# Layer 2's cross attention: outputs by token from centred folded values, six heads' maxima as the bias of the exponential, steps in a written order

## The chip, the core and the metric

The kernel runs on one core of a Trainium2 chip. The core's engines work from queues of their own: TensorE (PE in the profile; PEld are its weight loads) for matrix products, VectorE (DVE), ScalarE (ACT) and GpSimd (POOL) for the rest, and SyncE (SP), which issues most DMAs. Products land in PSUM, which has eight banks of 512 float32 per partition; all else lies in SBUF.

The metric is the device time of one execution in microseconds, as the median over runs. Everything is float32.

## The reference

A small decoder of four layers; every layer is a cross attention to a context, then a mixture of experts. The change concerns the attention of layer 2. Cut to what matters, with 8 sequences of 256 tokens of width 128 (2048 tokens, 16 tiles of 128), 64 context rows per sequence, 16 heads of width 64:

```python
q = split_heads(einsum('bnd,df->bnf', norm(x), Wq)) * 64 ** -0.5
k, v = split(einsum('bmc,cf->bmf', context, Wkv), 2)
k = concatenate((null_k, k)); v = concatenate((null_v, v))     # one null key and value per head
attn = softmax(einsum('bhid,bhjd->bhij', q, k))                # 65 numbers per head
out = einsum('bnf,fd->bnd', merge_heads(attn @ v), Wout)
mu, var = mean(out), variance(out)
out = (out - mu) * rsqrt(var + 1e-6) * ln_scale + ln_bias
x = x + tanh(gate) * out
```

`norm` is a layer norm over the 128 numbers of a token. What follows is layer 2's feed-forward part: two routings to 8 experts (cosine logits, a mask, a softmax over the chosen), an attention whose projections are mixed by the first routing's gates, and experts weighted by the second's.

## The kernel before

x stays in SBUF as 16 tiles of 128 tokens by 128, in four chunks of four tiles (`TPC`). Layer 2's keys and values are *folded*: with `Wq` and the keys multiplied beforehand (`G`, per sequence 128 x 16 heads x 64) the scores of a tile are one product of its normed, turned x with `G`; with the values and `Wout` multiplied beforehand (`U`) the output of a tile is one product of its weights with `U`. `folds` makes G and U in eight pieces (k = 0 to 7, two heads each): `keys_values(k)`, then `fold`. Five calls of it are spread over layer 1's experts (`l1_ffn`), the others run before `l2_xattn`. `constants2` does the same with the null key and value (`gn`, `nvu`).

`l2_xattn` then goes through the tiles:

- `normed(c)` norms a chunk and turns it (`xTs`).
- `weights(t)`, two tiles ahead: scores of 16 heads x 64 in two PSUM banks (`sc2`) and the null scores (`sn`) on PE; the maximum per head, the subtraction from all 1024 scores and from the null scores, on DVE; two exponentials on ACT; sums and reciprocal on DVE; the division (a multiplication by `rs`) on POOL.
- `turned(t)`: eight turns on PE, copied by ACT to `pTs` (two banks of kind `l2m` are shared by all such uses), and one turn of the null weights.
- `summed(b)`, for two tiles of one sequence: the output as 128 features x 256 tokens (`py2`), copied (`yT2`), turned back to tokens (`yt2`), statistics with `bn_stats` and `bn_aggr`, copied (`yr2`), `rstd` by a power on POOL, the norm on DVE, scale and bias on POOL, the addition to x on DVE.

Within the loop, at tiles 8 to 14, stands part of the next layer's work for chunks 0 and 1: `normed2` and `logits2` (norm, turn, cosine logits), `routed2` (mask and gates), `spread2` and `loaded2` (the gates go to HBM and come back spread over 128 partitions into the place of `G`). `l2_ffn` begins with `queries(0)`, which multiplies x's normed chunk by these gates.

The order on each engine: where the code says nothing, a scheduler of the framework orders the instructions of a stage when the program is built, by its own estimates. In a block with `tc.manual_schedule` every engine takes its instructions in the order of the code; layers 1 and 3 have such blocks, layer 2's attention has none. Waits between engines are semaphores that the framework sets from what each instruction reads and writes. `power` is the POOL instruction at line 219. `evac` copies PSUM to SBUF by ACT and DVE in turns. `over(a, n)` repeats a number along the last axis.

Of the kernel before, what the change touches and what calls it, by code (L numbers as in the profile page):

```python
# [20 lines left out]
AF = mybir.ActivationFunctionType  # L21
# [3 lines left out]
P = 128  # L25
# [3 lines left out]
NCH = 4  # L29
# [8 lines left out]
def tile_flamingo(ctx: ExitStack, tc: tile.TileContext, a: dict, out: bass.AP):  # L38
# [1365 lines left out]
    def normed2(c):  # L1404


        st = mk(small, [P, TPC, 6], "st")
        t = slice(c * TPC, (c + 1) * TPC)
        for k in range(TPC):
            v.bn_stats(st[:, k, :], xs(c)[:, k, :])  # L1410
            v.bn_aggr(r2["mv"][:, c * TPC + k, :], st[:, k, :])
        pw = mk(small, [P, 2, TPC], "pw")
        v.tensor_scalar(pw[:, 0], r2["mv"][:, t, 1], 1e-5, None, ALU.add)
        v.tensor_scalar(pw[:, 1], r2["mv"][:, t, 1], 1.0 + 1e-5, 1e-10, ALU.mult, ALU.add)
        power(r2["pw"][:, :, t], pw, 2 * TPC)
        xn = mk(act, [P, TPC, D], "xn")
        ln_apply(xn, xs(c), r2["mv"][:, t], r2["pw"][:, 1, t])
        return xn
# [26 lines left out]
    def routed2(half, i):  # L1445
# [7 lines left out]
        v.tensor_tensor(lo, lo, under(sgt[:, i, :], HT), ALU.subtract)  # L1453

# [5 lines left out]
        top = top_mask(lo, 2)  # L1460
        v.tensor_tensor(top, top, over(m, E), ALU.mult)
# [30 lines left out]
    def l1_l2():  # L1492

# [11 lines left out]
        with psum(4, 2), tc.tile_pool(name="l2w", bufs=1) as wp:  # L1505
# [35 lines left out]
            def constants2():  # L1541
# [14 lines left out]
                s.activation(gn, pn2, AF.Copy, scale=0.125)  # L1556
# [23 lines left out]
            def fold(k, kT, vd):  # L1580
                G, U = Gs[k // 4], Us[k // 4]
# [10 lines left out]
                for h in range(2):  # L1592
                    evac(G[:, :, 2 * (k % 4) + h, :], pg[:, h])
                for b4 in range(2):
# [11 lines left out]
            def folds():  # L1606


                with behind(l1["ph"]):
                    kv = keys_values(0)  # L1610
                yield
                for k in range(8):
                    nxt = keys_values(k + 1) if k < 7 else None
                    fold(k, *kv)
# [3 lines left out]
            def l2_xattn(lp):  # L1618

                p2s = [t.rearrange("p (h m) -> p h m", h=16) for t in (wa2[:, 0:1024], wa2[:, 1024:2048])]  # L1620
                p2s.append(vds[0].rearrange("p b t m -> p (b t m)").rearrange("p (h m) -> p h m", h=16))
                p2Ts = [wa2[:, 2048 * i : 2048 * (i + 1)].rearrange("p (k q) -> p k q", k=8) for i in (1, 2)]
                xTs, pTs, pnTs = {}, {}, {}

                def normed(c):
                    xTs[c] = mk(wp, [P, CW], "t2k", bufs=2)
                    pt = misc([P, CW], "pt")
                    xn = layernorm(c)
# [895 lines left out]
```

## Time and profile before

| what | value |
|---|---|
| median of six runs | 1112.53 us (1109.11 to 1125.4) |
| the profiled execution, its own time | 1101.95 us |
| its span, first to last instruction | 1100.2 us |
| mean granted TensorE clock | 0.93 |
| PE busy | 973.2 us (88%) |
| PEld busy | 550.4 us (50%) |
| DVE busy | 629.8 us (57%) |
| ACT busy | 451.2 us (41%) |
| POOL busy | 312.8 us (28%) |
| HBM traffic | 50.50 MB read, 8.26 MB written |

The span begins with the first instruction and ends with the last. Busy time is that in which an engine had an instruction running; PE's is drawn a little long, since products overlap and their ends are modelled. The profile has a view by windows of time, a view of groups of instructions (by line, engine, operation and tiles, with what ended the idle time ahead of them), a timeline, and a chain of waits: from the last instruction back, at each step to whatever released it. In these views the names of tiles that share an arena are those of the arena: `arena_a` stands for the weights `pa`, the turned weights and the folding's inputs; `t2k` for the turned x. A float32 product of 512 columns shows as two instructions.

Layer 2's attention proper lies between about 576 and 694 us of the span, the folding of pieces 4 to 7 directly ahead of it, layer 2's experts behind it.

### The profile page before, as it was taken

To read this page: it belongs to the slowest core of one execution; us is meant where nothing else is said; L and a number is where in the kernel's file an instruction comes from. 1 tells how busy PE (TensorE), PEld (TensorE's weight loads), DVE (VectorE), ACT (ScalarE), POOL (GpSimd) and SP (SyncE) were. 2 spreads that over 40 slices of the span, in tenths; PEclk is the share of its full clock that TensorE was granted. 3 is DMA by queue.
4 is the path that set the end of the run, shared out by engine and by line. 5 is a ranking of instruction groups with operands and counts; after the bars stand their busy time and mean duration, and the time that the engine had idled before them with its cause. 6 is when DMAs were issued, how large, how long until landed. Compare 5 with 4: busy or idle time off the path is not lost.

```text
span 1100.2 us, 14774 instructions
## 1 busy us (share of the span) xinstructions
PE 973.2 (88%) x5090; PEld 550.4 (50%) x5090; DVE 629.8 (57%) x1690; ACT 451.2 (41%) x875; POOL 312.8 (28%) x348
## 2 busy tenths in 40 slices
PE   5898989889999999899998988979998699887896
PEld 3557756644444344334454646434444244555684
DVE  4475435565746563343428997844757755555454
ACT  3633533354444455632234434322203444452353
POOL 2128761141100001000003555230541610322554
PEclk9889999999999998898999998989999899985698
DMA  9403321031010100300210000714431203000243
GB/s 252 89 13 52 75 57 32 25 96 38 3 39 4 41 2 2 115 0 1 77 39 1 1 0 7 244 38 154 154 114 54 101 22 133 1 20 11 45 85 101
DMA packets 59337, 64.31 MB, mean 58 GB/s; under 512 B 11096, under 2 KB 48512, under 8 KB 59008
## 3 DMA queue, kind: packets, MB, share of 16 engines
q1 hardware_dynamic: 54016, 54.14, 16.0%
q0 software_dynamic: 3968, 8.13, 3.7%
q10 hardware_dynamic: 1280, 1.09, 0.5%
q8 instruction: 42, 0.69, 0.3%
q14 instruction: 31, 0.25, 0.1%
HBM read 50.50 MB, written 8.26 MB: 53 GB/s over the span
## 4 chain that ended last, share of the span: by engine, by line
PE 65%; DVE 17%; POOL 6%; ACT 5%; issue 4%; DMA 2%; SPq 1%; ACTq 0%; POOLq 0%; DVEq 0%
PE gur L770 4%; PE st L1126 4%; PE pymT L1814 4%; PE yr L795 3%; PE sc L1032 2%; PE phm L1905 2%; DVE nmx L1039 2%; PE o L1145 2%; PE pqmT L1814 2%; PE yt L1349 2%; PE gu L746 2%; PE pvmT L1814 2%; PE sc L1640 2%; PE ph L1301 1%; PE pu L1597 1%
## 5 line engine op out<-in xcount | busy, mean ns | idle before, releaser
L219 POOL TENSOR_TENSOR rstd<-rstd,mhalf 128x4 f32<-128x4 f32 (+1 forms) x37 | 35.2, 950 | 377.6 <-DVE rstd L234 335.6
L1039 DVE TENSOR_REDUCE nmx<-sc 128x4 f32<-128x1024 f32 x64 | 76.5, 1220 | 56.5 <-PE sc L1032 56.4
L1130 ACT ACTIVATE pT<-st 128x1024 f32<-128x1024 f32 x64 | 64.5, 1023 | 63.7 <-PE st L1126 48.3
L770 PE MATMUL gur<-arena_a,xrT 128*128 x184 | 62.2, 462 | 0.9 <-ACT xrT L764 0.7
L612 POOL DMA_INDIRECT xr<-xk,dp_src x46 | 46.8, 1017 | 42.0 <-DVE lg_m L287 28.3
L1814 PE MATMUL pymT<-G,arena_b 128*128 128x512 f32 x104 | 47.2, 598 | 1.5 <-DVE G L1806 1.3
L1661 POOL TENSOR_TENSOR arena_a<-arena_a,rs 128x1024 f32<-128x1024 f32 x16 | 30.5, 1904 | 58.7 <-DVE rs L1660 42.3
L787 DVE COPY aTr<-pta 128x256 f32<-128x256 f32 x46 | 19.5, 424 | 47.6 <-PE pta L785 47.6
L795 PE MATMUL yr<-arena_a,aTr 128*128 (+1 forms) x276 | 38.4, 275 | 0.1
L770 PEld LDWEIGHTS gur<-arena_a,xrT 128*128 128x128 f32 x184 | 31.7, 190 | 13.3 <-ACT xrT L764 1.6
L1640 PE MATMUL sc<-G,t2k 128*128 128x512 f32 x64 | 34.2, 626 | 4.6 <-DVE rs L1659 3.7
L778 ACT ACTIVATE sgr<-gur 128x352 f32<-128x352 f32 x46 | 21.3, 463 | 37.1 <-PE gur L770 37.1
L612 POOL DMA_INDIRECT xn<-yg,dp_rows x32 | 30.3, 947 | 21.5 <-issue 7.9
L795 PEld LDWEIGHTS yr<-arena_a,aTr 128*128 128x128 f32 (+1 forms) x276 | 34.4, 191 | 0.3 <-DVE aTr L787 0.3
L1126 PE MATMUL st<-arena_a 32*128 32x512 f32 x128 | 34.2, 672 | 0.0
L275 DVE SCALAR_TENSOR_TENSOR x<-yt,tg,x 128x512 f32<-128x512 f32 x16 | 12.0, 748 | 37.6 <-PE yt L1354 21.6
L612 POOL DMA_INDIRECT xr<-z,dp_src x30 | 28.5, 950 | 15.4 <-issue 8.1
L1814 PEld LDWEIGHTS pymT<-G,arena_b 128*128 128x128 f32 x104 | 19.1, 190 | 26.1 <-issue 14.3
L2226 POOL TENSOR_TENSOR arena_a<-arena_a 128x256 f32<-128x256 f32 x18 | 14.0, 775 | 60.4 <-DVE arena_a L2225 60.4
L1032 PE MATMUL sc<-arena_b 32*128 32x512 f32 x128 | 30.2, 666 | 0.8 <-DVE yr L804 0.4
L1126 PE MATMUL st<-arena_b,l1k 32*128 32x512 f32 x128 | 30.9, 631 | 0.0
L1905 PE MATMUL phm<-nT,arena_b 128*128 128x512 f32 x64 | 29.9, 622 | 0.0
(544 smaller groups left out, 2395.8 us busy)
## 6 DMA issues: line engine op xcount, KB each, us to landing
G<-gd SPq DMA_DIRECT2D x40, 512.0 KB
xe<-gd SPq DMA_DIRECT2D x8, 512.0 KB
arena_a<-in_L_ffn_exp_wgu_dram SPq DMA_DIRECT2D x2, 1408.0 KB
yg<-yr SPq DMA_DIRECT2D x10, 256.0 KB
arena_a<-qkT SPq DMA_DIRECT2D x32, 64.0 KB
arena_a<-in_L_xattn_Wkv_dram SPq DMA_DIRECT2D x1, 2048.0 KB
y<-yr SPq DMA_DIRECT2D x6, 256.0 KB
x<-in_x_dram SPq DMA_DIRECT2D x4, 256.0 KB
```

Of the source, the lines that this page charges most:

```text
L219: g.tensor_tensor(dst, src, mhalf[:, 0:n], ALU.pow)
L612: return g.indirect_dma_start(out=dst, out_offset=None, in_=src, in_offset=bass.IndirectOffsetOnAxis(ap=idx, axis=0))
L770: pe.matmul(gu[:, h, 0:352], xrT[t], wgu[:, bass.ds(e + 1, 1), h * 352 : h * 352 + 352].rearrange("p e f -> p (e f)"), start=True, stop=True,)
L795: pe.matmul(y, aT[0:n, i, :], wd[0:n, bass.ds(e + 1, 1), i, :].rearrange("p e d -> p (e d)"), start=(i == 0), stop=(i == 2),)
L1032: pe.matmul(sc[:, i].rearrange("p h t -> p (h t)"), qd[r, k, tokens(qt)], kb[r, k, b].rearrange("p h t -> p (h t)"), start=True, stop=True,)
L1039: v.tensor_reduce(nmx[:, qt, 2 * u : 2 * u + 2, 2 * k : 2 * k + 2], sc, AX.X, ALU.max, negate=True)
L1126: pe.matmul(st[:, i], kd[r, k, b, kt * P : (kt + 1) * P], qb[r, k, :, tb], start=True, stop=True)
L1130: s.activation(pT[n, u], st, AF.Exp)
L1640: pe.matmul(sc[:, 8 * k : 8 * k + 8, :].rearrange("p h m -> p (h m)"), xT[:, q], Gs[k][:, b].rearrange("p h m -> p (h m)"), start=True, st ...
L1661: g.tensor_tensor(pa, pa, over(rs, S2), ALU.mult)
L1814: last_pe[0] = pe.matmul(pq, w[:, e, :], xe[e // 4][:, e % 4, :], start=(e == 0), stop=(e == E - 1))
L1905: pe.matmul(ph, w1p[:, e, :], nTc(c), start=True, stop=True)
```

## The change

It does five things.

1. **Folded values less their means.** The mean over the 128 output columns is taken off `wo` (and so off `U` and `nvu`), in `folds`. The output then has mean zero, and its variance is the mean of its squares: `bn_stats` and `bn_aggr` go.
2. **Outputs by token.** `summed(t)` takes the turned weights as the stationary side and U as the moving one, for one tile at a time: the output is tokens x 128, four tiles in one bank `y`. The copies and turns behind it go. ACT's `squared` sums the squares, `rstd` takes the power per pair, `back` scales from PSUM on DVE and adds to x on POOL. The bias is added to x in `normed`.
3. **Six heads' maxima as the bias.** For heads 0 to 5 ACT takes the exponential from PSUM with the negated maximum as its bias and sums it as it goes (`accum_out`); for heads 6 to 15 and the null weights, which now lie behind them in one stretch of `pa`, DVE subtracts as before and ACT takes one exponential.
4. **Steps of fixed order.** `l2_xattn` stands in a `manual_schedule` block. Step t holds the pieces of tiles t+2, t+1, t, t-1 and a finished pair, in one written order; norms, logits, routing and the spread of gates are cut into pieces (`routed2` becomes a generator, `normed2` two functions) and appended to the end of chosen steps (`plan`). The norms of chunks 0 and 1 stand ahead of the block.
5. **Last folding within.** `fold` is cut in two; the values of k = 6 and 7 are folded in steps -2 and -1.

The null scores and the turned null weights share one bank (`null`). `gn` changes sign, so that `min` with the negated maxima serves. The diff, cut to its core:

```diff
             def folds():
                 with behind(l1["ph"]):
                     kv = keys_values(0)
+                wm = mk(small, [P, 8], "wm", bufs=1)
+                row_sum(wm, wo)
+                v.tensor_scalar(wm, wm, 1.0 / D, None, ALU.mult)
+                g.tensor_tensor(wo, wo, over(wm, D), ALU.subtract)
                 yield
...
+                    fold_scores(k, kT)
+                    if k < 6:
+                        fold_values(k, vd)
...
+                def scores(t):
...
+                    pe.matmul(sn(t), xT[:, q], gn, start=True, stop=True)
...
+                def maxima(t):
...
+                    v.tensor_reduce(nm, sc, AX.X, ALU.max, negate=True)
+                    v.tensor_tensor(nm, nm, sn(t), ALU.min)
+                    v.tensor_tensor(pa[:, HB:16, :], sc[:, HB:16, :], over(nm[:, HB:16], S2), ALU.add)
+                    v.tensor_tensor(pn, nm, sn(t), ALU.subtract)
+
+                def exps(t):
...
+                    for h in range(HB):
+                        s.activation(
+                            pa[:, h, :], sc[:, h, :], AF.Exp, bias=nm[:, h : h + 1], accum_out=rs[:, h : h + 1]
+                        )
+                    pl = pas[t % 3][:, HB * S2 : 1040]
+                    s.activation(pl, pl, AF.Exp)
+
+                def divided(t):
...
+                    row_sum(rs[:, HB:16], pa[:, HB:16, :])
                     v.tensor_tensor(rs, rs, pn, ALU.add)
                     v.reciprocal(rs, rs)
+                    g.tensor_tensor(pn, pn, rs, ALU.mult)
                     g.tensor_tensor(pa, pa, over(rs, S2), ALU.mult)
...
+                def summed(t):
+
+                    yt = y[:, t % TPC, :]
                     for k in range(8):
+                        pe.matmul(yt, pTs[t % 2][:, k, :], Us[k // 4][:, t // 2, k % 4, :], start=(k == 0), stop=False)
+                    pe.matmul(yt, pnTs.pop(t), nvu, start=False, stop=True)
+
+                def squared(t):
+                    junk = mk(lp, [P, D], "junk2")
+                    s.activation(junk, y[:, t % TPC, :], AF.Square, scale=D**-0.5, accum_out=vs[:, t : t + 1])
...
+                def back(b):
                     yn = mk(lp, [P, 2, D], "yn")
+                    for t in (2 * b, 2 * b + 1):
+                        v.scalar_tensor_tensor(
+                            yn[:, t % 2, :], y[:, t % TPC, :], vs[:, t : t + 1], lns, ALU.mult, ALU.mult
                         )
                     xb = x[:, 2 * b : 2 * b + 2, :]
+                    g.tensor_tensor(xb, xb, yn, ALU.add)
...
+                for k in (6, 7):
+                    plan[k - 8].append(lambda k=k: fold_values(k, vds[k % 2]))
+                for c, t in ((2, 1), (3, 4)):
+                    stats, apply, turn = normed(c)
...
+                def late(c):
+                    stats, apply = normed2(c)
...
+                    def turn_in():
+                        got.extend(logits2(c, apply(), 0, misc, nsq))
+                        got[0]()
+
+                    return stats, turn_in, lambda: got[1]()
+
+                for c, t in ((0, 6), (1, 10)):
+                    for k, f in enumerate(late(c)):
+                        plan[t + k].append(f)
+                routing = routed2(0, 0)
+                for t in (12, 13, 14):
+                    plan[t].append(lambda: next(routing, None))
...
+                plan[15].append(first_half)
+                for t in range(-2, NT + 2):
                     if t + 2 < NT:
+                        scores(t + 2)
+                    done = t - 2 if t >= 3 and t % 2 else None
+                    if 0 <= t + 1 < NT:
+                        divided(t + 1)
+                    if done:
+                        rstd(done // 2)
+                    if 0 <= t < NT:
+                        turned(t)
+                    if t + 2 < NT:
+                        maxima(t + 2)
+                        exps(t + 2)
+                    if 0 <= t - 1 < NT:
+                        summed(t - 1)
+                        squared(t - 1)
+                    if done:
+                        back(done // 2)
+                    for f in plan[t]:
+                        f()
...
+                with tc.manual_schedule(engines=all_four):
+                    l2_xattn(xp)
```

`first_half` is the old `t == 14` branch: `spread2` for chunks 0 and 1, then `loaded2` for both. `turned(t)` turns the null weights first, then the eight blocks, and copies all three results on ACT.

## The prediction

> **What bounds it now.** I read the page's 40 slices first: PE is nine tenths busy nearly everywhere, and DVE reaches nine tenths only in the stretch from 576 to 690 us, the attention of layer 2, which the change rewrites. So I cut that stretch and the start of the next layer into windows (columns: length, then busy time and instructions of PE, PEld, DVE, ACT, POOL, then granted clock, DMA share, GB/s):
>
> ```profile
> 576.00:590.00 14.00, 9.21 (x27) 4.52 (x28) 10.18 (x18) 3.81 (x6) 2.18 (x3) 0.90 0.00 0
> 590.00:635.00 45.00, 43.95 (x209) 29.10 (x207) 40.03 (x90) 22.66 (x49) 24.65 (x26) 0.99 0.00 1
> 635.00:684.00 49.00, 41.03 (x179) 24.78 (x180) 41.87 (x128) 21.15 (x47) 26.32 (x27) 0.92 0.00 1
> ...
> 716.00:733.00 17.00, 10.07 (x33) 3.83 (x32) 4.61 (x8) 3.73 (x7) 7.52 (x9) 0.70 0.15 51
> ```
>
> The filling (576 to 590) leaves PE 5 us idle; then PE is full, and DVE nearly; after 635 neither is full. The chain of waits, cut to 590 to 625 us, says which of the two paces the full part (start, length, what):
>
> ```profile
> by line: PE sc L1640 33.3%; PE py L1685 29.6%; PE tp L1675 18.7%; PE py L1686 5.4%; PE sn L1647 3.8%; PE tn L1678 2.3%; PE yt L1691 1.9%; ACT arena_a L1676 1.7%; PE pt L1630 1.2%; ACT yr L1698 1.0%; issue 0.5%; DVE rstd L1700 0.5%; ACT pn L
> ...
> 605.32 3.46 PE py L1685 x16
> 608.77 0.62 PE py L1686 x2
> ```
>
> It is PE. One pair of tiles costs it 2 x (1.72 scores + 0.13 null scores + 0.95 turns + 0.11) + 4.08 outputs + 0.22 = 10.1 us, 5.06 a tile. The exponentials of tiles 0 to 10 (L1655) start at 581.07 and 634.48: 5.34 a tile. The last five tiles take 43.9 us, to 678.34: routing falls there. Then the groups of 574 to 700 us (count, busy us, mean ns, idle before and releaser):
>
> ```profile
> L287 DVE TENSOR_REDUCE m<-sc 128x16 f32<-128x1024 f32 x16 | 19.4, 1214 | 4.7 <-PE sc L1640 4.7
> L316 DVE TENSOR_REDUCE rs<-arena_a 128x16 f32<-128x1024 f32 x16 | 19.4, 1210 | 2.0 <-ACT arena_a L1655 2.0
> L1653 DVE TENSOR_TENSOR arena_a<-sc,m 128x1024 f32<-128x1024 f32 x16 | 19.2, 1199 | 0.1
> L1661 POOL TENSOR_TENSOR arena_a<-arena_a,rs 128x1024 f32<-128x1024 f32 x16 | 30.5, 1904 | 58.7 <-DVE rs L1660 42.3 <-DVE pn L1654 4.0 <-DVE tk_m L305 3.4
> L1698 ACT COPY yr<-yt 128x256 f32<-128x256 f32 x8 | 2.9, 367 | 1.2 <-DVE st L1695 1.2
> ```
>
> Three passes over 1024 numbers fill DVE. The last line matters later: ACT's copy of `yt` waits for DVE's statistics of the same `yt`, though neither writes what the other reads. Two readers of one PSUM bank go one after the other here.
>
> **The change, part by part.** PE: the sixteen `py` products of 256 columns and the two turns become per tile 18 instructions on 128 columns. `pu` (L1597) has that form: 16 in 1.98 us, 0.124 each. So 2.23 a tile against (4.08 + 0.22) / 2 = 2.15: PE stays at 1.85 + 1.06 + 2.23 = 5.14 a tile. PE gains nothing, so what can be won is idle time only: the 5 us of filling and about 17 us of the last tiles (43.9 - 5 x 5.34).
>
> DVE: heads 6 to 15 alone are shifted and summed, 640 of 1024 numbers. A 1024-wide pass is 1.13 us from start to start (619.19 to 620.33), about 0.07 of it fixed, so 640 take 0.74 (0.80 to its end). Statistics leave (`bn_stats`, `bn_aggr`), `yn` takes one pass per tile from PSUM, and the addition to x goes to POOL. That removes this collision, POOL and DVE in one stretch of the timeline (the usual addition takes 0.43):
>
> ```profile
> 628.21 1.90 POOL L1661 TENSOR_TENSOR arena_a<-arena_a,rs 128x1024 f32<-128x1024 f32 x1
> 628.29 2.10 DVE L1710 TENSOR_TENSOR x<-x,yn 128x256 f32<-128x256 f32 x1 [0.20 <-POOL yn L1708]
> ```
>
> ACT: the copies `yT` and `yr` leave (0.37 each, per pair). Six exponentials of 64 columns with a bias and a sum come in, then one of 656 (0.73, by 1.058 for 1024), and a square with its sum (0.42). What one small exponential costs is not in the trace; the nearest rows are these:
>
> ```profile
> 14.16 0.41 ACT L413 ACTIVATE sg<-arena_b 64x256 f32<-64x256 f32 x1 [2.77 <-DMA arena_b<-in_ctx_dram]
> 14.48 0.18 ACT L413 ACTIVATION_READ_ACCUMULATOR sg<-arena_b 64x1 f32 x1
> 14.69 0.42 ACT L413 ACTIVATE sg<-arena_b 64x256 f32<-64x256 f32 x1
> ...
> 761.30 0.40 ACT L1869 ACTIVATE pam<-pam,mm 128x128 f32<-128x128 f32 x1 [3.30 <-DVE mm L1868]
> 761.60 0.19 ACT L1869 ACTIVATION_READ_ACCUMULATOR pam<-pam,mm 128x1 f32 x1
> 761.70 0.49 ACT L1869 ACTIVATE pam<-pam,mm 128x256 f32<-128x256 f32 x1
> ```
>
> Each sum is a second instruction. The lower pair is the same exponential with bias, 0.40 apart at 128 columns, 0.34 at 64; the upper is 0.53 apart at 256 columns, 0.37 at 64 and about 0.45 with a bias. I take 0.39, six in 2.34.
>
> [...]
>
> **The fixed order makes a loop.** In every step each engine takes: DVE `divided(t+1)`, then `maxima(t+2)`; ACT the copies, `exps(t+2)`, `squared(t-1)`. DVE can't sum tile t+1 before ACT ends `exps(t+1)`, can't start the maxima of t+2 before that sum, and ACT can't start `exps(t+2)` before the shifted heads are written, since both read the first bank of `sc`. Once round: sum 0.74, add 0.09, reciprocal 0.16, maximum 1.13, minimum 0.09, shift 0.80 = 3.01 on DVE, 2.34 + 0.73 = 3.07 on ACT, two waits of 0.04: 6.15 us, above PE's 5.14 and the old 5.34. (Between 5.8 and 6.5 by the price of the small exponentials.) Fifteen rounds lead from the end of the first tile's exponentials to the last's: 92.2.
>
> Added to single rounds: in odd steps `back` reads bank `y` on DVE behind ACT's `squared` in the same bank (0.45 after the exponentials) and takes 0.6 for two tiles (L642, 0.346 for 128 columns); the next sum is queued behind it: 1.1 in five rounds, 5.5. The planned pieces stand last in a step, so what they wait for holds the next step's work. Applying the norm in step 5: four passes behind `back`, partly against POOL's addition, 1.5. `turn_in` in steps 7 and 11: PE's turns wait for that pass, and the next scores (1.85) queue behind them on PE: 3.1 each. `logits` in step 8: PE's second turn waits for an ACT copy behind `exps(10)`, so scores 11 come 2.8 late. Step 12: the first piece of routing waits on DVE for those logits and POOL's power (1.65), with the sum of tile 14 behind it: 4.4. Together 14.9. Sum 92.2 + 5.5 + 14.9 = 112.6, against 97.3 now (exponentials end at 582.13 and 679.40): **+15.3**. Bounds: 87 with stalls covered by idle DVE, to 118.
>
> Start: the four `pu` groups of k = 6, 7 (4 us on PE) go into the filling. The last `pg` ends at 573.1 less 2.0, G is copied by 572.5, scores, maximum and shift (2.0 + 2.1) and exponentials (3.0) end near 579.6: **-2.5**.
>
> Tail (same view; the spread of the gates, their loads, the first gated product):
>
> ```profile
> 684.63 1.08 SPq L1478 DMA_DIRECT2D gd<-arena_a  x2
> ...
> 686.17 4.14 SPq L1487 DMA_DIRECT2D G<-gd  x8
> ...
> 690.17 0.69 DVE L1806 TENSOR_TENSOR G<-G,nT 128x512 f32<-128x512 f32 x1 [0.58 <-DMA G<-gd]
> ```
>
> Now 10.8 us pass from the last exponentials to the first gated product; PE works on outputs under the loads. After, the spread stands at the end of step 15: `back` 1.05, routing 2.0, sum 1.0, POOL 2.2, turns 1.1, outputs of tile 14 2.3, spread 0.9, copies 0.9 = 11.4, and 4.8 from the last copy to the product as now (685.41 to 690.17): 16.2, **+5.4**; 0 if the pieces overlap. Only tile 15's outputs lie under these loads, so SP's queue starts them later against the end.
>
> Layer 2's experts: PE idles 7 of 17 us at 716 to 733, because x's last tiles are ready at 698.8, 8.6 after the first gated product, and their norm, routing and squares (POOL, 721) come late. After, x is ready before that product: 0 to 7 won, I take **-4**, the middle, since the program's own order there decides. Taken at nothing: the means of `wo` (1.21 on DVE, 1.90 on POOL, the L316 and L1661 forms) run under the matmuls of layer 1's experts, where POOL is idle; without that cover 3.1, and the first `pu` would be late.
>
> Sum: +15.3 - 2.5 + 5.4 - 4 = +14.2. The profiled execution took 1101.95 (span 1100.2), 1% under the median 1112.53; on its own time 1116, on the median **1126 us**.
>
> **Rivals.** *PE paces.* If the small exponentials cost near 0.22, or started at the minimum, the loop would fall below 5.14 and PE would set 15 x 5.14 = 77 plus 8 of planned matmuls: 85 against 97.3, -12.3; with -2.5 + 5.4 - 4 it is -13, **1099**. For it: DVE does 3.5 a step instead of 5.3, and loses no time to POOL. Against: the 0.40 row, and `yr` waiting for `st`. *Stalls covered.* The loop holds, but DVE's 3 us of idle time in every round take in the planned pieces: 92.2 + 5.5 - 97.3 = 0.4; with the other three terms -0.7, **1112**. *Table loads.* If the square needs another table than the exponential, two loads of 1.28 a tile stand in the loop: 16 x 2.57 = 41 more, **1167**. Against it: the squares at 10.89 follow a tanh at 10.78 with no load between. This is slower still than my forecast. The changed steps plainly do what they say; no rival is needed for that.
>
> **Chances.** Loop with stalls 0.49, covered 0.28, PE paces 0.20, table loads 0.03. About 1% (11 us) is what a measurement here can tell from no change. The first case lies mostly above 1124, the second within, the third straddles 1101 with two thirds below plus a little of the second: faster 0.18, same 0.34, slower 0.48. The range leaves out a tenth at each end: 1098 (PE paces) to 1141 (6.5 a round and no recovery). The likeliest case alone: 1117 to 1141.
>
> **What would show it.** The changed profile should have exponential blocks 6.15 apart in steps without extras, PE with idle time in each step, DVE waiting for ACT's 656-wide exponential and ACT for DVE's shift; gaps of 9 to 10 us at tiles 10, 11, 14, 15; an ACT read per small exponential. A chain made of PE lines, 5.2 apart, or ACT starting its exponentials before the shift ends, proves the loop wrong.

## The result, and the profile after

The changed kernel takes 1142.13 us (median of 20 runs, 1134.4 to 1151.44), the kernel before 1113.98 us (median of 46). The ratio is **1.0251, 95% interval 1.0227 to 1.0274**: 28 us slower. Ratios leave out executions more than 1.5% above the fastest of the same kernel, so they can differ from the quotient of the medians. The prediction said 1126 us, 1098 to 1141: the side was right, the size was half of what came, and the time lies 1 us outside the range.

The profiled execution after took 1148.32 us (span 1146.4, clock 0.907), against 1101.95 before. Of these 46 us, 12 lie ahead of all changed code: layer 1's experts begin at 443.7 us before and at 456.0 after. In the profiles of the experiments below on chips on which before takes about 1115 us, with the same code there, they begin between 445 and 458. So this part comes and goes with the execution, and stretches are measured from here on from their own beginnings:

| stretch | before | after |
|---|---|---|
| layer 1's experts begin, to the first tile's wide exponential | 137.4 | 139.0 |
| from there to the last tile's wide exponential (starts) | 97.3 | 117.1 |
| from there until x is complete (last addition to x ends) | 20.4 | 24.2 |
| from the last wide exponential to the first gated product | 11.8 | 29.1 |
| x complete, to the end of the span | 401.5 | 410.1 |

The windows of the new attention (length, then busy time and instructions of PE, PEld, DVE, ACT, POOL, then granted clock, DMA share, GB/s; the filling, tiles 1 to 9, tiles 10 to 15, the tail):

```profile
587.00:602.00 15.00, 10.97 (x51) 7.33 (x50) 7.44 (x15) 7.71 (x31) 2.08 (x2) 0.91 0.00 0
602.00:655.00 53.00, 43.13 (x250) 30.65 (x249) 36.44 (x100) 31.44 (x138) 26.31 (x26) 0.96 0.00 1
655.00:713.00 58.00, 43.34 (x231) 29.82 (x231) 28.00 (x77) 29.00 (x124) 21.97 (x22) 0.87 0.00 1
713.00:742.00 29.00, 14.04 (x72) 12.31 (x72) 15.22 (x65) 9.66 (x29) 9.16 (x9) 0.62 0.28 91
```

Nothing is full any more. PE, which had 43.95 of 45 us before, has 43.13 of 53; DVE fell from 0.89 of the stretch to 0.69, and ACT has 0.59 (0.50 before). That is what a circle of waits looks like: every engine idle a part of each round. The chain of waits says so (start, length, what; one whole round):

```profile
607.55 0.65 ACT arena_a L1692
608.22 0.83 DVE rs L316
609.08 0.19 DVE rs L1698
609.29 0.25 DVE rs L1699
609.54 1.09 DVE m L1678
610.72 0.18 DVE m L1679
611.00 0.82 DVE arena_a L1680
611.92 0.35 ACT arena_a L1688 x2
612.42 1.38 ACT arena_a L1688 x9
613.80 0.65 ACT arena_a L1692
```

PE, which made the chain before, does not appear in such a round. It runs from one wide exponential (L1692) to the next, 6.25 us: 0.67 for it, then DVE's sum, addition, reciprocal, maximum, minimum and shift until 611.92 (3.70), then the six small exponentials (1.88). The groups of 588 to 742 us (count, busy us, mean ns, idle before and releaser) put numbers to the two waits:

```profile
L1688 ACT ACTIVATE arena_a<-sc,m 128x64 f32<-128x64 f32 x96 | 28.7, 317 | 31.2 <-DVE arena_a L1681 28.3 <-DVE arena_a L1680 2.9
L316 DVE TENSOR_REDUCE rs<-arena_a 128x10 f32<-128x640 f32 x16 | 13.0, 813 | 13.3 <-ACT arena_a L1692 13.3
L1740 DVE SCALAR_TENSOR_TENSOR yn<-y,vs,arena_a 128x128 f32<-128x128 f32 x16 | 4.9, 346 | 23.1 <-ACT junk L1730 16.5 <-ACT pnT L1717 5.8 <-POOL vs L219 0.8
```

ACT waits 31.2 us for DVE's shift, DVE 13.3 for ACT's wide exponential, and another 23.1 in the scaling of finished pairs, most of it for ACT's square.

### The profile page after: what moved, and what is told of

Same layout as the page of the kernel before. It is cut to its first block, busy times and chain, and to the rows that moved or that the text cites. A ratio compares the mean times of both kernels' runs of the same rounds, so it can differ in the third digit from the quotient of the medians.

```text
span 1146.4 us, 15229 instructions
## 1 busy us (share of the span) xinstructions
PE 989.4 (86%) x5218; PEld 571.8 (50%) x5218; DVE 610.0 (53%) x1650; ACT 472.0 (41%) x1069; POOL 310.7 (27%) x345
## 4 chain that ended last, share of the span: by engine, by line
PE 61%; DVE 16%; ACT 9%; DMA 4%; POOL 4%; issue 3%; SPq 2%; ACTq 0%; DVEq 0%; POOLq 0%
PE gur L770 4%; PE st L1126 4%; PE pymT L1905 3%; PE yr L795 3%; PE pqmT L1905 2%; PE pvmT L1905 2%; PE sc L1032 2%; PE phm L1996 2%; ACT arena_a L1688 2%; PE o L1145 2%; PE pkmT L1905 2%; PE yt L1349 2%; PE gu L746 2%; PE ph L1301 2%; DVE nmx L1039 2%
## 5 line engine op out<-in xcount | busy, mean ns | idle before, releaser
L219 POOL TENSOR_TENSOR rstd<-rstd,mhalf 128x4 f32<-128x4 f32 (+1 forms) x29 | 29.2, 1007 | 338.6 <-DVE rstd L234 308.0
L770 PE MATMUL gur<-arena_a,xrT 128*128 x184 | 65.0, 479 | 0.9 <-ACT xrT L764 0.7
L1688 ACT ACTIVATE arena_a<-sc,m 128x64 f32<-128x64 f32 x96 | 28.7, 317 | 31.2 <-DVE arena_a L1681 28.3
L1665 PE MATMUL sc<-G,xT 128*128 128x512 f32 x64 | 37.9, 723 | 0.0
L1725 PE MATMUL y<-U,arena_a 128*128 128x128 f32 x256 | 34.8, 294 | 2.9 <-DVE on L1464 2.2
L612 POOL DMA_INDIRECT xn<-yg,dp_rows x32 | 30.3, 947 | 25.4 <-PE gu L746 9.0
L1905 PE MATMUL pvmT<-G,arena_b 128*128 128x512 f32 x56 | 27.0, 637 | 10.0 <-DVE G L1897 10.0
L1725 PEld LDWEIGHTS y<-U,arena_a 128*128 128x128 f32 x256 | 33.1, 209 | 3.6 <-ACT arena_a L1719 3.0
L1126 PE MATMUL st<-arena_b,l1k 32*128 32x512 f32 x128 | 34.1, 684 | 0.0
L1032 PE MATMUL sc<-arena_b 32*128 32x512 f32 x128 | 32.9, 723 | 0.8 <-DVE yr L804 0.4
L275 DVE SCALAR_TENSOR_TENSOR x<-yt,tg,x 128x512 f32<-128x512 f32 x16 | 12.0, 748 | 40.6 <-PE yt L1354 22.9
```

The costliest lines, as they stand in the source:

```text
L219: g.tensor_tensor(dst, src, mhalf[:, 0:n], ALU.pow)
L612: return g.indirect_dma_start(out=dst, out_offset=None, in_=src, in_offset=bass.IndirectOffsetOnAxis(ap=idx, axis=0))
L770: pe.matmul(gu[:, h, 0:352], xrT[t], wgu[:, bass.ds(e + 1, 1), h * 352 : h * 352 + 352].rearrange("p e f -> p (e f)"), start=True, stop=True,)
L1032: pe.matmul(sc[:, i].rearrange("p h t -> p (h t)"), qd[r, k, tokens(qt)], kb[r, k, b].rearrange("p h t -> p (h t)"), start=True, stop=True,)
L1126: pe.matmul(st[:, i], kd[r, k, b, kt * P : (kt + 1) * P], qb[r, k, :, tb], start=True, stop=True)
L1665: pe.matmul(sc[:, 8 * k : 8 * k + 8, :].rearrange("p h m -> p (h m)"), xT[:, q], Gs[k][:, b].rearrange("p h m -> p (h m)"), start=True, st ...
```

## The experiments

All are edits of the changed kernel. A ratio is to the kernel before, run beside it on the same chip. Four of them ran on a chip on which before itself takes 1193 us; there only ratios and the changed stretches compare. The table gathers what the profiles show; "rounds" is from the first to the last wide exponential, the next two columns count from the start of the last one. The expectations count from its end, 0.7 to 0.8 us later.

| kernel | rounds | to x complete | to first gated product | x complete to end | ratio, 95% interval |
|---|---|---|---|---|---|
| before | 97.3 | 20.4 | 11.8 | 401.5 | 1 |
| after | 117.1 | 24.2 | 29.1 | 410.1 | 1.0251, 1.0227 to 1.0274 |
| all heads shifted | 108.0 | 25.0 | 30.6 | 407.2 | 1.0198, 1.0111 to 1.0286 |
| maxima first | 147.3 | 25.1 | 29.6 | 406.7 | 1.0546, 1.0464 to 1.0628 |
| free order | 85.0 | 19.1 | 23.6 | 406.8 | 1.0009, 0.9938 to 1.0079 |
| free order, again | 86.8 | 20.3 | 24.9 | 407.8 | 0.9887, 0.9847 to 0.9927 |
| next layer held | 114.7 | 20.4 | 22.0 | 412.8 | 1.0272, 1.0189 to 1.0356 |
| sum last (slow chip) | 107.5 | 23.9 | 28.4 | 432.6 | 1.0188, 1.0089 to 1.0288 |
| gates first (slow chip) | 117.1 | 26.8 | 21.8 | 432.9 | 1.0275, 1.0201 to 1.0349 |
| free order, all heads (slow chip) | 84.6 | 20.1 | 25.3 | 434.9 | 0.9895, 0.9834 to 0.9956 |
| logits cut finer (slow chip) | 112.1 | 23.9 | 28.4 | 434.9 | 1.0173, 1.0081 to 1.0265 |
| reordered | 92.4 | 22.9 | 21.6 | 402.2 | 0.9970, 0.9939 to 1.0001 |
| both ends of the tail | 117.1 | 26.2 | 25.0 | 408.2 | 1.0230, 1.0186 to 1.0273 |
| reordered, gates last | 92.4 | 19.7 | 23.8 | 415.3 | 1.0010, 0.9976 to 1.0044 |

**All heads shifted.** Is it the circle or DVE's amount of work?

```diff
-                HB = 6
+                HB = 0
```

> The changed kernel with no head's maximum as a bias: all 16 heads shifted by DVE, one exponential of 1040, the sum over 16 heads on DVE. Loop theory (DVE's sum, maximum, shift and ACT's exponentials follow each other in one circle, 6.25 us a plain round in the changed kernel's trace): ACT's part falls from 6 x 0.29 + 0.65 = 2.4 to about 1.07, DVE's grows by 2 x 0.39 = 0.78, so a plain round is 6.25 - 1.33 + 0.78 = 5.7, 15 rounds give back 8 us, and the time is about 1134. Rival (DVE's amount of work sets the rounds, not the circle): 15 x 0.78 = 12 us slower, 1154. Rival (PE paces, the waits are hidden): no change, 1142, intervals as before.

The plain rounds became 5.47, 5.55 and 5.67 us, the whole stretch 9.1 us shorter, and the time 1131.11 us against 1113.79. So DVE got more work and the rounds got shorter, by what the loop theory said: the circle paces, DVE's load does not. Within the written order the six heads' bias costs time in the rounds; the two whole ratios, 1.0198 and 1.0251, have intervals that overlap.

**Maxima first.** The circle cut by moving DVE's sum and ACT's copies behind the next tile's maxima and exponentials.

```diff
+                    if t + 2 < NT:
+                        maxima(t + 2)
+                        exps(t + 2)
                     if 0 <= t + 1 < NT:
                         divided(t + 1)
...
                         turned(t)
-                    if t + 2 < NT:
-                        maxima(t + 2)
-                        exps(t + 2)
```

> The changed kernel with one block of the step moved: the maxima and exponentials of tile t+2 stand ahead of the sum and division of tile t+1 and the turns of tile t. The same work, but the sum no longer stands between one tile's exponentials and the next tile's maxima. Loop theory: the circle is broken, PE paces plain rounds at 5.2 to 5.4 instead of 6.25, and the time falls by 15 x 0.9 = 13 us or a little less (planned pieces still hold their steps), to 1129 to 1133. Rival (the work on DVE and ACT, or the two banks of the scores, paces): no change. Rival (ACT's copies of the turned weights now queue behind the exponentials, and outputs come late): slower by up to 10.

The time was 1172.2 us: a miss, on the side of the last rival and beyond it. PE's timeline shows what took the circle's place (start, length, what, and in brackets the idle time before it and its releaser):

```profile
603.12 0.61 PE L1663 MATMUL null<-gn,xT 128*128 128x16 f32 x2 [1.07 <-ACT pnT L1717]
603.57 3.76 PE L1665 MATMUL sc<-G,xT 128*128 128x512 f32 x4
610.02 0.37 PE L1708 MATMUL null<-ident,arena_a 128*16 128x128 f32 x1 [2.69 <-DVE arena_a L1681]
```

With ACT's copy of the turned null weights behind the exponentials, the next null scores, which go into the same bank (and the scores behind them on PE), wait for that copy: a longer circle, exponentials, copy, scores, maximum, shift, of about 9.8 us a round. A bank of their own for the turned null weights was not tried, so this circle is read from the waits and not proved by an edit. The granted clock in 600 to 640 us was 0.77, and one set of scores took 3.76 us instead of 1.96.

**Sum last.** The same cut, with the copies left where they were.

```diff
-                    if 0 <= t + 1 < NT:
-                        divided(t + 1)
...
                         exps(t + 2)
+                    if 0 <= t + 1 < NT:
+                        divided(t + 1)
```

> The changed kernel with one piece of the step moved: the sum and division of tile t+1 stand behind the exponentials of tile t+2; the turns of tile t and their copies keep their place ahead of those exponentials. In the run with the maxima first, ACT's copies had slid behind the exponentials, and PE's scores (which write the bank that the copy of the turned null weights reads) waited for them; here they do not. Loop theory (the circle through DVE's sum costs): plain rounds 5.3 where no finished pair is scaled, 6.2 where it is (DVE's scaling still waits for ACT's square behind the exponentials), so from the first tile's to the last's exponentials about 105 us instead of 117, time 1130. Rival (the wait on the shared null bank is what paces the changed kernel too): rounds of 6.2 everywhere, 1142. Rival (as the run with the maxima first): above 1160.

Rounds are 5.23 and 5.16 us where nothing else is in the step, 5.85 to 7.3 with a finished pair or a norm, still 10 to 11.7 with the planned logits; 107.5 in all, 9.6 of the expected 12 us. On the same chip the two kernels with the old step kept their plain rounds of 6.25 us, so rounds compare between the chips.

**Logits cut finer.** The planned pieces of chunk 0 (statistics, norm, turn, products, turn back) one step apart each; `logits2` gives its second half as two functions.

```diff
...
+                    if c == 0:
+                        return (
+                            stats,
+                            lambda: got.extend(logits2(c, apply(), 0, misc, nsq)),
+                            lambda: got[0](),
+                            lambda: got[1](),
+                            lambda: got[2](),
+                        )
...
```

> The changed kernel with chunk 0's planned pieces cut finer: the norm stays in step 7, its turn goes to step 8, its logits' products to step 9, the turn back to step 10. In the changed kernel's trace these pieces make intervals of 11.8 and 8.4 us at tiles 10 and 11, against 6.25 of a plain round. Theory that PE queues in order behind a turn that waits for the norm of the same step: the two fall to about 8 and 6.3, 5 to 6 us less, and the time is about 1136. Rival (another piece waits in its place, or the norm's own time on DVE holds the next sum): 1141 to 1143.

The intervals at tiles 10 and 11 fell from 11.78 and 8.37 us to 8.45 and 6.95, the stretch by 5.0. Chunk 1's pieces, left as they were, kept theirs (11.76, 10.09). So it was PE's queue behind the turn, as the prediction had it.

**Next layer held.** In the changed kernel the scheduler puts pieces of the next layer between the written instructions, since a written order fixes only how these stand to each other. This run keeps them out (`shift` is the residual's L1878; the mask's preparation is held likewise).

```diff
...
             run_all(qs[0])
             with tc.issue_after(behind[0]):
+                for c in (2, 3):
+                    stats, apply = normed2(c)
+                    stats()
+                    xn2.append(apply())
+                for c in (0, 1):
+                    shift(c)
...
```

> The changed kernel with pieces of the next layer kept out of the block: the norms of chunks 2 and 3, the residual's shift of chunks 0 and 1 and the mask's preparation are held on DVE behind the first gated product. In the changed kernel's trace they stand between the written instructions: twice a wait of 1.76 us on POOL's power within the loop, about 4 us between the exponentials of the last tile and its sum, and 3.7 us (the last norm) ahead of the first gated product. Theory that these strangers made the tail long: last exponentials to first gated product 20 to 22 us instead of 28.4, each of the two steps in the loop 1.2 shorter, in all 8 to 10 us less, of which layer 2's experts give back 0 to 4 since their norms come later: 1134 to 1140. Rival (the tail is long because routing itself and the division of the last tile follow each other): within 2 us of 1142.

Ahead of the experts it came as expected and more: 22.0 us from the last exponential to the first gated product instead of 29.1, and 2.4 less in the rounds. At the end little is seen of it, where 1134 to 1140 had been expected: 1140.65 us, with a ratio of 1.0272 from four executions, too wide in its interval to tell a gain of 6 us. The window from 20 to 40 us behind the first gated product, and PE's longest pause in it, show where some of it may have gone:

```profile
748.45:768.45 20.00, 10.32 (x28) 3.62 (x27) 9.62 (x22) 5.96 (x13) 8.66 (x11) 0.69 0.17 52
```

```profile
761.56 1.91 PE L1441 MATMUL pl<-nsq,ones 128*32 128x512 f32 x2 [7.21 <-POOL nsq L1436]
```

PE is idle for 9.7 us there. For 7.21 of them it waits for POOL's squares of the second routing, and POOL has nine pieces of layer 3's weights (L2331 to L2334, 753.09 to 760.5) ahead of these. It is not the late norms that PE waits for: they end at 738.2 and 742.7. In the changed kernel the same POOL pieces fall under products of PE (16.7 of the 20 us of the like window are busy); which of the held pieces moved them apart is not shown.

**Gates first.** The spread of the gates and their loads at the head of step 15.

```diff
-                plan[15].append(first_half)
...
+                    if t == 15:
+                        first_half()
```

> The changed kernel with the spread of the gates and their loads put at the head of step 15 instead of its end, so that PE turns the gates ahead of the last tile's weights and of the outputs of tile 14, which wait for POOL's division. Theory that this queue is part of the long tail: the loads are issued 4 to 5 us earlier, the first gated product follows by 4. Whether the end follows is the question: the run with the norms held back lost in the experts all that it had won ahead of them. If the experts start earlier and keep it: 1138. If layer 2's experts are paced by the norms of the last tiles: 1142.

The first gated product came 7.3 us earlier than in the changed kernel, x was complete 2.6 later (tile 14's outputs now stand behind the gates on PE, and DVE's scaling waited 6.59 us for their square), and the ratio did not move: 1.0275.

**Both ends of the tail.** Gates first, the last tile's sum ahead of the scaling and of routing, and the first gated product behind the last scaling.

```diff
...
+                    if t + 2 == NT - 1:
+                        divided(NT - 1)
...
```

> The changed kernel with both ends of the tail moved at once: the spread of the gates at the head of step 15 (which alone gave nothing), the last tile's sum and division in step 13 directly behind its exponentials, ahead of the scaling of a pair and of routing on DVE, and the first gated product held behind the last pair's scaling. Theory that layer 2's experts wait for two things, the gates and the complete x, and that the run with the gates alone won nothing because x came no earlier: x complete 17 to 19 us after the last exponentials (23.6 in the changed kernel), gates after 22 to 24 (28.4), and the end 5 us earlier: ratio 1.019 to 1.022 where the changed kernel has 1.025. Rival (the tail is not what sets the end, the experts are): ratio as the changed kernel, 1.024 to 1.028.

A miss: x was complete 25.4 us after the end of the last exponentials, the first gated product came 24.2 after it, and the ratio 1.023 can be told neither from the changed kernel's nor from the expected 1.019 to 1.022. PE's turn of the gates now waits 6.03 us for routing, with the last tile's turns and tile 14's outputs queued behind it. Whether an earlier x alone would be worth its time stays open here.

**Free order.** The block of fixed order taken away, nothing else; then the same with all heads shifted, and once more with more rounds.

```diff
-                with tc.manual_schedule(engines=all_four):
-                    l2_xattn(xp)
+                l2_xattn(xp)
```

> The changed kernel without the block of fixed order around layer 2's attention: the same instructions, ordered by the scheduler. If the fixed order is what costs (rounds of 6.25, stalls of 15 us by planned pieces, a tail of 28 us instead of 11), the time falls by 20 to 35 us, to 1107 to 1122, and the changed arithmetic itself is worth nothing or a small gain against before. If the arithmetic costs (six exponentials with sums on ACT, outputs by token), it stays above 1130. Which of the two holds is open; I lean to the first, at 1115.

> The changed kernel without the fixed order and without the six heads' bias (all 16 heads shifted by DVE): what centred values and outputs by token are worth alone. DVE then has about 4.4 us a tile (three passes of 1.13 and the rest), still below PE's 5.14, so if PE paces a freely ordered kernel the six heads are worth nothing and the time is that of the run without fixed order, 1105 within 4. If DVE's passes still held PE up there, as in the kernel before, it is 1110 to 1115.

> The changed kernel without the fixed order, once more and with more rounds, beside the kernel before on the same chip: by the medians of the first such run 0.8% faster than before, while the interval there reached from 0.994 to 1.008. If the gain is real (x is complete before the first gated product, so layer 2's experts lose no time to the norms): 0.985 to 0.997. If it was noise: 0.998 to 1.005.

By the medians 1104.78 us against 1113.79 in the first run (less than the expected 1107 to 1122; but the ratio, 1.0009, has an interval that spans 1 and rests on five executions of before), and 1106.24 against 1117.17 in the repeat, ratio 0.9887. Against the changed kernel that is a clear gain, and the repeat is 1.1% faster than before as well, as expected of a real gain; since the two intervals do not overlap, the size of this second gain stays open. The exponentials of all tiles take 85.0 and 86.8 us from first to last, and PE is nearly full again (the windows of the repeat, columns as above, and the head of its chain of waits for 600 to 640 us):

```profile
600.00:680.00 80.00, 76.14 (x470) 55.57 (x468) 58.88 (x147) 58.33 (x255) 43.69 (x44) 0.98 0.00 1
680.00:705.00 25.00, 11.71 (x71) 10.34 (x71) 15.36 (x67) 9.92 (x30) 9.24 (x9) 0.78 0.29 100
```

```profile
by line: PE sc L1665 19.0%; PE y L1725 14.5%; DVE m L1678 10.3%; PE tp L1714 9.8%; POOL arena_a L1701 9.4%; DVE arena_a L1680 5.2%; issue 4.9%; POOL pw_n L219 4.1%; PE y L1726 4.1%; DVE rs L316 3.9%; DVE pw L1415 2.5%; DVE xn L240 2.2%; DVE
```

PE is busy for 76.14 of 80 us, but the chain is not made of PE alone: PE's lines have about half of it, DVE and POOL most of the rest.

With all heads shifted it is 0.9895, on another chip: in free order the six heads' bias is worth nothing that these intervals show.

**Reordered.** The changed arithmetic in another written order, built from the runs above. Ahead of the lines shown stand `rstd` and `turned(t)`; `inner` holds the planned turns and the spread of the gates.

```diff
                         scores(t + 2)
...
+                    for f in inner[t]:
+                        f()
+                    if t + 2 < NT:
+                        maxima(t + 2)
+                    if 0 <= t - 1 < NT:
+                        summed(t - 1)
+                        squared(t - 1)
+                    if t + 2 < NT:
+                        exps(t + 2)
+                    if 0 <= t + 1 < NT:
+                        divided(t + 1)
+                    if done:
+                        back(done // 2)
+                    for f in plan[t]:
+                        f()
```

> The changed kernel's arithmetic in another written order, with what the earlier runs showed taken together: in each step the sum and division of tile t+1 last; the square of tile t-1 ahead of the exponentials on ACT, so that the scaling of a finished pair does not wait behind them; the planned norm, turn, products and turn back one step apart, with turns behind the tile's own turns; all of routing's later pieces behind the last tile's sum; the spread of the gates ahead of tile 14's outputs; the exponential's table loaded by a dummy ahead of the block; the next layer's norms, shifts and mask, and its first gated product, held behind the routing, the first gated product or the last pair's scaling. Loop theory: PE paces, 5.3 to 5.8 a round, 80 to 90 us from the first tile's exponentials to the last's (117 in the changed kernel, 85 in free order); from the last exponentials x is complete after 13 to 15 us (23.6) and the first gated product follows after 18 to 20 (28.4). In all 0.965 to 0.975 of the changed kernel, 0.99 to 1.00 of the one before. Rival (fixed order costs by itself, since no written order fits every stall): first to last exponentials stay above 100, and the time is above 1.01 of before.

0.997: 3% below the changed kernel, level with before. Plain rounds are 5.22 to 5.32 us, near PE's 5.14; steps with norms or logits take 6.1 to 7.3, and the 92.4 in all lie a little above the expected 80 to 90. The rival as it was stated (above 100 us, above 1.01) falls with this, though free order still has the shorter rounds in all. The expected tail did not come: x complete 22.1 us after the end of the last exponentials, not 13 to 15. PE's timeline:

```profile
693.43 1.86 PE L1496 MATMUL pg<-ident,w 128*8 128x128 f32 x8 [4.96 <-DVE vs L1747]
695.09 2.93 PE L1738 MATMUL y<-U,arena_a 128*128 128x128 f32 x16
699.69 2.02 PE L1738 MATMUL y<-U,arena_a 128*128 128x128 f32 x16 [1.25 <-DVE yn L1753]
```

The gates' turn waits for routing with both last outputs behind it. So the outputs were put ahead of it:

```diff
-                inner[15].append(first_half)
...
                         squared(t - 1)
+                        if t == 16:
+                            first_half()
```

> The reordered kernel with the spread of the gates and their loads put behind the outputs and the square of tile 15, and every shift of the next layer's residual held behind the first gated product. In the trace of the reordered kernel PE's turn of the gates stood 4.96 us waiting for routing, with the outputs of tiles 14 and 15 queued behind it, so x was complete 22 us after the last exponentials instead of the 13 to 15 that were expected of it, and the first gated product was held until then. Theory: routing ends as late as there, so the gates' turn starts no later, while the outputs go ahead of it: x complete 14 to 17 us after the last exponentials, the first gated product 18 to 20 after them instead of 21.6, the end 2 to 5 us earlier: 0.992 to 0.995 of before, where the reordered kernel had 0.997. Rival (the experts wait for something else): as the reordered kernel, 0.996 to 0.999.

A miss too: 1.001. The outputs of tile 15 now waited themselves:

```profile
700.21 3.75 PE L1738 MATMUL y<-U,arena_a 128*128 128x128 f32 x16 [4.31 <-DVE mv_n L1413]
```

They go into the bank `y`, which DVE's scaling of tiles 12 and 13 reads, and that scaling stood behind all of routing on DVE, ending at 700.06. x was complete 3 us earlier, not 5 to 8; and from there to the end it took 415.3 us instead of 402.2. Some of that comes early in the experts: from 732 to 752 us PE works 14.15 of 20 at a clock of 0.69, where the reordered kernel has 16.36 at 1.00 in the like window. Whether the residual's shifts, held longer, are the reason is not shown.

## Why the prediction was right or wrong

**What bounds before; PE gains nothing.** Right, as far as it goes: in free order PE is nearly full (76.14 of 80 us), and the rounds take 85.0 and 86.8 us in all. That is the figure of the rival "PE paces", 85, and the repeat came to 0.9887 of before, as that rival's 1099 against 1112.53 had it (0.988). This agreement is partly luck: against before, the tail is 12 to 13 us longer there, not 5.4, and the experts are 7 to 8 shorter, not 4; and the first run of it gave 1.0009. What the rival had wrong was the condition: not a quicker small exponential brings it, but the absence of the fixed order.

**The fixed order makes a loop.** Right in mechanism, order of engines and size: 6.15 forecast, 6.25 measured. Its two halves were both off and cancelled, so that the total fits so closely is luck. DVE's half was put at 3.01 us and takes 3.70: from start to start the minimum, addition and reciprocal take 0.28, 0.21 and 0.25 instead of 0.09, 0.09 and 0.16, the sum and the shift 0.86 and 0.92 instead of 0.74 and 0.80. ACT's half was put at 3.07 and takes 2.55. Six small exponentials were put at 2.34 (0.39 each) and start 0.29 apart, as one round's rows show (the read of a sum lies beside the two exponentials around it):

```profile
612.22 0.30 ACT L1688 ACTIVATE arena_a<-sc,m 128x64 f32<-128x64 f32 x1
612.42 0.20 ACT L1688 ACTIVATION_READ_ACCUMULATOR arena_a<-sc,m 128x1 f32 x1
612.51 0.31 ACT L1688 ACTIVATE arena_a<-sc,m 128x64 f32<-128x64 f32 x1
```

The reads take 0.19 to 0.23. The prediction worked its 0.39 out from longer rows, 0.34 from one pair and 0.45 from the other; the 0.08 that it put on for a bias in the second is what its rows of 256 columns differ by (0.49 with a bias, 0.41 without). The measured 0.29 lies below both.

**Planned pieces.** Right in kind, a little small. The intervals with `turn_in` are 11.78 us, the one with the logits 8.37, the one ahead of the last tile 10.09: 5.5, 5.5, 2.1 and 3.8 above a plain round, where 3.1, 3.1, 2.8 and 4.4 were forecast. The `turn_in` steps are the odd ones, so `back` (0.8) is in them too. Unforeseen were the scheduler's own insertions: the residual's shift (L1878) twice, waiting on DVE for POOL's power, 1.1 us a time; the run that held them out won 2.4. First to last exponential: **+15.3 forecast, +19.8 measured**.

**Start.** Wrong, by little: -2.5 forecast, +1.3 measured (by the exponentials' ends, as there). The exponential's table is now loaded between the first tile's shift and its exponential:

```profile
591.97 1.28 ACT L1688 ACT_TABLE_LOAD   x1 [4.17 <-issue]
593.26 0.31 ACT L1688 ACTIVATE arena_a<-sc,m 128x64 f32<-128x64 f32 x1
```

That is 1.28 of the 3.8 between them (before, the load ran at 576.22, ahead of the first shift); the rest is of the size by which this stretch varies between profiles (136.1 to 139.2 in kernels with the same code there). The reordered kernels were meant to load it ahead by a dummy, but there the load stands in the same place:

```profile
587.26 1.28 ACT L1701 ACT_TABLE_LOAD   x1 [4.16 <-issue]
```

In the trace of the reordered kernel the dummy ran at 19.20 us, outside the block, and nine table loads came between it and this one. What an early load is worth was not measured.

**Tail: the mis-sized term.** +5.4 was forecast from the end of the last exponentials to the first gated product; it is +17.5 (10.8 to 28.3). The forecast's list of queued steps was right, but three of them are longer. The sum of tile 15, behind `back` and routing on DVE, ends its reciprocal 8.7 us after the exponentials where 4.05 were forecast: the next layer's norm of chunk 2 stands between routing's instructions, with a wait for POOL. The last tile's turns and tile 14's outputs took 2.5 us more on PE, at a granted clock of 0.50. And from the gates' last copy to the first product it took 9.7 us instead of 4.8: the mask's load stood ahead of the gates' loads, and the norm of chunk 3, waiting for POOL's power, ahead of the product. The first and the last of these, in the timeline of DVE and of SP's queue:

```profile
717.69 0.35 DVE L240 TENSOR_SCALAR xn<-x,mv_n,pw_n 128x128 f32<-128x128 f32 x1 [1.64 <-POOL pw_n L219]
720.28 0.81 DVE L316 TENSOR_REDUCE rs<-arena_a 128x10 f32<-128x640 f32 x1
740.13 1.11 DVE L240 TENSOR_SCALAR xn<-x,mv_n,pw_n 128x128 f32<-128x128 f32 x4 [1.54 <-POOL pw_n L219]
741.16 2.49 DVE L1897 TENSOR_TENSOR G<-G,nT 128x512 f32<-128x512 f32 x4
```

```profile
733.03 0.37 SPq L1855 DMA_DIRECT2D mi<-in_mask_BxS_ik_dram  x1
733.50 4.17 SPq L1495 DMA_DIRECT2D G<-gd  x8
```

The run that held the next layer's pieces back puts a price on them: 22.0 us instead of 29.1, counted from the start of the last exponentials.

The step behind it failed as well: the prediction took the first gated product for the point from which the end follows. The experts also need all of x. Two runs brought the gates 7 us earlier, one with x later, one with other work of the next layer later, and neither ended measurably earlier. Closer to the time comes the rounds plus the way to a complete x: 141.3 us in the changed kernel, 117.7 before, 107.1 in free order, 115.2 reordered, with ratios of 1.025, 1, 0.989 and 0.997. The 23.6 us between the first two are most of the 28. It is no rule: with the gates last it is 112.1, 5.6 less than before, and the ratio is 1.0010 with an interval from 0.9976; there the experts lost what had been won ahead of them.

From the beginning of layer 1's experts the terms measure +19.8 + 1.3 + 17.5 - 4.8 = +33.8 between the two profiled executions, where +14.2 was forecast, and 12.1 of the 19.6 between these are the tail's. The medians lie 28 apart, so some of the 33.8 belongs to the two executions.

**Layer 2's experts.** Counted from the first gated product, 4.8 us were won where 4 were forecast, for the reason given: x is complete before that product (736.3 against 741.2). Counted from x, the experts take 8.6 longer, as they now wait for the gates. These are two sides of one thing, and the gain is no gain of time.

**Means of `wo`.** Taken at nothing; no run puts a price on them, since the stretch they lie in varies by as much as the 3.1 us in question.

**What would show it.** The blocks 6.25 apart, PE idle in each step, ACT and DVE waiting for each other, gaps at tiles 10, 11, 14 and 15, one read per small exponential: all are there. The exponential's table is loaded once between 588 and 742 us (1.28 us, at 591.97), not in each round, so the rival of the table loads falls; that of the covered stalls falls with the intervals above. The gaps are 11.78, 8.37, 11.78 and 10.09 us where 9 to 10 were forecast.

## What to carry to other kernels

When an order is written by hand for several engines, follow one round of it from any instruction back to itself, through every queue and every shared bank; if that circle is longer than the busiest engine's work, the order is the bound, and moving one piece behind another can be worth more than making any piece quicker. A written order fixes only its own instructions: whatever the scheduler may put between them, and the waits that come along, belongs in the sum. And before pricing a tail by one milestone, ask what else its successor needs; here gates that came 7 us earlier were worth nothing that could be measured.

## What the hardware showed that was not expected

PE's clock fell to half at 712, with no pause of PE above 1.16 us in the four microseconds ahead. In the windows of four microseconds ahead of and in the tail (columns as above) it goes from 1.00 to 0.50 at 712 and is still there in the last one, in which PE works throughout:

```profile
708.00:712.00 4.00, 2.57 (x19) 1.92 (x18) 2.17 (x4) 1.68 (x12) 2.73 (x3) 1.00 0.01 2
712.00:716.00 4.00, 2.04 (x9) 2.08 (x10) 2.29 (x15) 2.15 (x8) 0.72 (x1) 0.50 0.00 0
716.00:720.00 4.00, 2.43 (x11) 1.91 (x9) 2.29 (x13) 0.37 (x2) 1.65 (x1) 0.50 0.00 2
720.00:724.00 4.00, 0.46 (x2) 0.17 (x3) 3.74 (x10) 0.02 (x1) 2.13 (x2) 0.50 0.00 0
724.00:728.00 4.00, 4.00 (x19) 4.00 (x20) 0.95 (x5) 1.55 (x4) 0.70 (x1) 0.50 0.00 0
```

Sixteen outputs that take 1.95 us at full clock took 3.75 at 713.96 and 3.55 at 725.68. When the clock fell, PE had worked 2.57 of the last 4 us: there was a pause of 1.16 us from 709.29, and one of 2.22 had only just begun, at 711.73. A longer pause, 3.64 us up to 722.07, came later, at half the clock already. What made the clock fall is not shown.
